# Graph attention in four layers: two of sixteen weight tiles of a unit made by ScalarE and GpSimd

## The chip, the cores and the metric

The kernel runs on one core of a Trainium2 chip. The core has five engines that each work through a queue of their own, in order: PE (TensorE, matrix products), DVE (VectorE), ACT (ScalarE), POOL (GpSimd) and SP, which here issues DMAs. They wait for each other by semaphores. The metric is the device time of one execution in microseconds (us); lower is better.

## The reference

There are 8 batches of 2048 nodes with 64 features, and one adjacency matrix `adj` of 2048 x 2048 zeros and ones. Four layers follow each other, each inside `x = layernorm(x + layer(x, adj))`. Layers 0, 1 and 2 are graph attention:

```python
h = x @ W                                    # layer 0 scales x and normalizes h as well
s1, s2 = h @ a[:64], h @ a[64:]
e = leaky_relu(s1[:, :, None] + s2[:, None, :], 0.2)
att = softmax(where(adj > 0, e, -big), axis=-1)
out = elu(att @ h)                           # layer 0 adds h; layer 2 has relu in place of elu
```

Layer 3 is a softmax per feature over the neighbours, without scores between pairs of nodes. The attention weights, 2048 x 2048 for each batch and each of three layers, are the bulk of the work.

## The kernel before

A **unit** is one layer and one batch. The list `todo` has 24 of them: layers 0 and 1 for batches 0 to 3, then layers 0 and 1 for batches 4 to 7, then layer 2 for all batches. Units are numbered n from 0, so n = 1 to 15 are the units of layers 0 and 1 after the very first; in this text (1,7) is the unit of layer 1 and batch 7. Layer 3 (`l3_products`, `p_l` in the profile) runs between the units of layer 2 and after them.

A unit's weights are made in K = 16 **tiles**: tile `jb` holds 128 source nodes on the partitions and all 2048 target nodes along the free dimension. In layers 0 and 1 a weight is exp of a leaky relu, and as exp(max(a, b)) = max(exp a, exp b), and a factor common to a row cancels in the softmax, a tile is one DVE instruction on exponentials that were taken of vectors before: `max(row, column) * edge`. Here `row` is `s.r` (name `r`, 128 x 2048 fp32, the same values in all partitions), the column is `s.e[:, 1, jb]` (name `se`), and `edge` is the mask as fp8, kept in SBUF. From n = 1 on, `r` lies in PSUM[...]. `spread` puts it there for each unit with four small PE products (`r<-row,ones`) after DVE's last tile of the unit before. In unit 0 the row lies in SBUF.

`weights(u, jb)` issues the DVE instruction into one of four buffers of the name `w`. `products(u, jb)` then issues four PE products of 512 columns (each is two instructions in the profile) that accumulate into `acc` in PSUM. The main loop runs over the units and, inside, over jb. At each jb it calls `reach`, which issues the weights up to this tile, then `products`, then one step of every background generator in `bg` (`bg.step`). These generators do everything else, some pieces at each tile:

- `finish` for the unit just done: ACT copies `acc` to `oT`, PE transposes it (`p_o`), DVE takes reciprocals `den`, ACT scales into `o`, POOL adds (`hb`, `eh`, `o`), ACT squares (`sq_x`), DVE sums (`st_x`), POOL takes a power (`st_x<-isw_x,mhalf`), ACT writes the new rows `x`.
- `scores` and `features0` for units to come: transposes, `h`, `xs`, `y`, scores, exponentials `se`, the row as three bf16 parts `rT3`, which goes to DRAM and comes back as `row`.
- `mask_out`, from unit 9 on: ACT copies the mask to fp32 (`mf`), SP writes it to DRAM for layer 3. The `raw`/`mf` buffers are four of 128 x 1024 each.

All instructions of PE, DVE, ACT and POOL go through a wrapper that keeps the program's order, so that nearly every row of the profile has line 80; one goes by the names of the tiles. Inside an engine the order of the program is the order of execution. The order between engines comes from semaphores, set from which instruction reads or writes which buffer.

Of the kernel before, what the change touches and what calls it, by code (L numbers as in the profile page):

```python
# [8 lines left out]
F32 = mybir.dt.float32  # L9
# [4 lines left out]
I32 = mybir.dt.int32  # L14
AF = mybir.ActivationFunctionType
ALU = mybir.AluOpType
AX = mybir.AxisListType

P = 128
# [31 lines left out]
def gnn4_kernel(ctx: ExitStack, tc: tile.TileContext, t, out):  # L51
    nc = tc.nc
    x_in, adjT = t["x"], t["adjT"]
    B, N, F = x_in.shape
    K = N // P
    K2 = K // 2
# [7 lines left out]
    small = ctx.enter_context(tc.tile_pool(name="small", bufs=2))  # L64
# [42 lines left out]
    class Banks:  # L107
# [4 lines left out]
        pool = None  # L112
        stack = None

        @classmethod
        def use(cls, name, bufs):
            if cls.stack is not None:
                cls.stack.close()
            cls.stack = ExitStack()
            cls.pool = cls.stack.enter_context(tc.tile_pool(name=name, bufs=bufs, space=PSUM))  # L120
# [20 lines left out]
    pe, dve, act, pool = (InOrder(e) for e in (nc.tensor, nc.vector, nc.scalar, nc.gpsimd))  # L141
# [58 lines left out]
    early = early_.enter_context(tc.tile_pool(name="early", bufs=3))  # L200
# [49 lines left out]
    edge = consts.tile([P, K, N], FP8, name="edge")  # L250
# [9 lines left out]
    half_ldeg = consts.tile([P, K], F32, name="half_ldeg")  # L260
    raws = {}

    AT_W = (0, 1, 2, 3, 6, 7, 8, 9)

    def load_raw(jb):

        if jb in AT_W:
            r = work.tile([P, N], I32, tag="w", name=f"raw_{jb}", bufs=4)
            nc.sync.dma_start(r, adjT[jb * P : (jb + 1) * P])
            raws[jb] = [r[:, : N // 2], r[:, N // 2 :]]  # L270
        elif jb < K:
            raws[jb] = []
            for h in range(2):
                r = early.tile([P, N // 2], I32, tag="raw", name=f"raw_{jb}_{h}", bufs=4)
                nc.sync.dma_start(
                    r, adjT[jb * P : (jb + 1) * P, h * (N // 2) : (h + 1) * (N // 2)]
                )
                raws[jb].append(r)
# [31 lines left out]
    def mask_out():  # L310

        for jb in range(K):
            for h in range(2):
                while not 3 < now[2] < K - 1:
                    yield 1
                r = early.tile([P, K2, P], F32, tag="raw", name=f"mf_{jb}_{h}", bufs=4)
                act.copy(
                    r,
                    edge[:, jb, h * (N // 2) : (h + 1) * (N // 2)].rearrange(
                        "p (i c) -> p i c", c=P  # L320
                    ),
                )
                nc.sync.dma_start(
                    mask_d[h * K2 : (h + 1) * K2, :, jb].rearrange("i p c -> p i c"), r
                )
                yield 2
# [22 lines left out]
    for jb in range(4):  # L349
        load_raw(jb)  # L350
# [204 lines left out]
    def exponentials(sc, s1, s2, s, layer, b, n):  # L555

        sc.e = small.tile([P, 3, K], F32, tag="se", name=f"se_{n}", bufs=B + 1)
        for i, v, scale in ((0, s1, 1.0 - ALPHA), (1, s2, ALPHA - 1.0), (2, s2, 1.0)):
            act.activation(sc.e[:, i], v, AF.Exp, scale=scale)

        def top():
            dve.tensor_reduce(
                s_top[:, layer, b : b + 1],
                s,
                AX.XY,
                ALU.max,
                apply_absolute_value=True,
            )

        return top  # L570
# [336 lines left out]
    def unit(layer, b):  # L907
        u = Unit()
        u.layer, u.b, u.n = layer, b, f"{layer}_{b}"
        u.s, u.w = S[layer, b], {}  # L910
        return u
# [4 lines left out]
    def halves(u, jb):  # L916
        parts = 2 if jb in (0, K - 1) and in_psum(u.layer, u.b) else 1
        return [slice(c * (N // parts), (c + 1) * (N // parts)) for c in range(parts)]

    def weights(u, jb):  # L920

        s = u.s
        w = u.w[jb] = work.tile([P, N], F32, tag="w", name=f"w_{u.n}_{jb}", bufs=4)
        low = s.low if u.layer == 2 else s.e[:, 1]
        for sl in halves(u, jb):
            dve.scalar_tensor_tensor(
                w[:, sl], s.r[:, sl], low[:, jb : jb + 1], edge[:, jb, sl], ALU.max, ALU.mult
            )

    def exponential(u, jb):  # L930

        w = u.w[jb]
        for sl in halves(u, jb):
            act.activation(w[:, sl], w[:, sl], AF.Exp, bias=u.s.down[:, jb : jb + 1])

    units, prepared, spreads = [], set(), {0}

    def spread_for(n):
        if n in spreads:
            return  # L940
        spreads.add(n)
        if n == 1:
            Banks.use("psR", 1)
            Banks.r = Banks.pool.tile([P, N], F32, tag="b", name="r")
        spread(*todo[n])
# [3 lines left out]
    def reach(t):  # L949

        while front[0] < K * len(todo):
            n, jb = divmod(front[0], K)
            layer, b = todo[n]
            if n not in prepared or front[0] > t + (2 if layer == 2 else 0):
                break
            if jb == 0:
                spread_for(n)
                units.append(unit(layer, b))
            weights(units[n], jb)
            front[0] += 1  # L960
            if jb == K - 1 and n + 1 in prepared:
                spread_for(n + 1)
        while behind[0] < min(front[0], t + 2):
            n, jb = divmod(behind[0], K)
            if todo[n][0] == 2:
                exponential(units[n], jb)
            behind[0] += 1

    def products(u, jb):

        s, w = u.s, u.w[jb]
        sums = [u.acc[c // 2][F * (c % 2) : F * (c % 2) + F, :] for c in range(NCH)]
        for c in range(NCH):
            pe.matmul(
                sums[c],
                lhsT=s.v[:, jb, :],
                rhs=w[:, c * 512 : (c + 1) * 512],
                start=(jb == 0),
                stop=False,
            )  # L980
        if jb == K - 1:

            assert s.whole
            for c in range(NCH):
                rows = slice(32 * c, 32 * c + 3)
                pe.matmul(sums[c], lhsT=s.mean[rows], rhs=emptyT[rows], start=False, stop=True)
# [341 lines left out]
    todo = [(layer, b) for half in (0, NB) for layer in (0, 1) for b in range(half, half + NB)]  # L1328
# [42 lines left out]
    begin = {0: 2, 1: 3, 4: 4, 5: 5, 6: 6, 8: 7}  # L1371
    for n, (layer, b) in enumerate(todo):
        if (layer, b) == (2, 1):
            early_.close()
            late = ctx.enter_context(tc.tile_pool(name="late", bufs=1))
            bg.add(l3_products())
        if (layer, b) == (2, 5):
            bg.add(flags())
        now[:] = layer, n, 0
        nxt = todo[n + 1] if n + 1 < len(todo) else None  # L1380
        done = nxt is None

        for jb in range(K):
            if n == 0:
                while masks < min(K, 9 + jb):
                    mask(p_deg, masks)
                    masks += 1
                    if masks == K:
                        empties(p_deg)
            now[2] = jb  # L1390
            reach(K * n + jb)
            u = units[n]
            if jb == 0:
                sums_of(u)
            products(u, jb)
            if jb == K - 1:
                end = [lambda u=u: finish(u)]
                if layer < 2:
                    end += [2 if now[0] < 2 else 1, lambda layer=layer, b=b: scores(layer + 1, b)]
                else:  # L1400
                    end += [1, lambda b=b: l3_features(b)]
                if layer == 1 and b % NB == NB - 1:
                    end += [lambda b=b: group(b // NB)]
                bg.add(chain(*end), begun=True)
            elif not done and jb >= 10 and ready(*nxt):
                prepare(*nxt)
                prepared.add(n + 1)
                done = True
            if layer == 0 and jb == 2 and 6 <= b + 4 < B:
                load_x(b + 4)  # L1410
            if n == 0 and jb == 3:
                bg.add(constants())
            if n == 9 and jb == 3:
                bg.add(mask_out())
            if jb == (1 if n < 2 else 4) and n in begin:
                bg.add(features0(begin[n]))
            bg.step()
        while not done:
            bg.step()
            if ready(*nxt):  # L1420
                prepare(*nxt)
                prepared.add(n + 1)
                done = True
# [509 lines left out]
```

## Time and profile before

| | us |
|---|---|
| device time, median of 3 runs (lowest, highest) | 1441.37 (1436.22, 1441.79) |
| the profiled execution, device time | 1439.37 |
| its span, first to last instruction | 1437.6 |
| PE busy in the span | 1238.5 (86%) |
| DVE busy | 1260.6 (88%) |
| ACT busy | 820.3 (57%) |
| POOL busy | 548.0 (38%) |
| units 1 to 15, between the first and the sixteenth spread of `r` | 107 to 781 |

A row of the profile's groups names the engine and operation, the tile written and those read, shapes and count, then busy time, the mean of one in ns, the idle time of the engine just before such instructions, and who ended that idle time. The rows of busy time by stretch give, after the stretch's length, busy us and count of instructions for PE, PE's weight loads, DVE, ACT and POOL, then the granted clock of PE, the share of the DMA engines, and GB/s. Rows of the timeline give start, duration, engine and instruction, several alike merged, and in brackets the idle time before. A busy PE is a model of pipelined products, and so a little generous.

### The profile page before, as it was taken

Reading aid. Unit: us, or ns where it says so; the run is one execution under the profiler, and the core shown is the slowest. Engines: PE = TensorE matmul, PEld = TensorE weight load, DVE = VectorE, ACT = ScalarE, POOL = GpSimd, SP = SyncE. Lnnn points to the kernel's source line nnn. Section 1 sums busy time; section 2 is a strip of 40 time slices with the busy share of each in tenths; the row PEclk is TensorE's granted clock in tenths of the full one; section 3 lists DMA queues with packets and bytes.
Section 4 is the critical chain, followed back from the end, with each engine's and each line's share of the span. In section 5 each row is a group of like instructions: output and inputs, shape, how many; then the busy total and the mean of one; then the engine's idle time right before and its main releaser. Section 6 shows DMA issues by size and latency. Waiting matters only on the chain.

```text
span 1437.6 us, 19117 instructions
## 1 busy us (share of the span) xinstructions
PE 1238.5 (86%) x7138; PEld 620.0 (43%) x7138; DVE 1260.6 (88%) x1260; ACT 820.3 (57%) x1585; POOL 548.0 (38%) x619
## 2 busy tenths in 40 slices
PE   3578788988899988999998887879999898988996
PEld 2323233333233333344332332336665464647996
DVE  4699889997899999999999898898989988878976
ACT  4415444664557545654533986787677766675442
POOL 1152463324423344331322211312445534367665
PEclk9988999999999999999999897999999998989998
DMA  8740000000000022221201000005453354531111
GB/s 297 249 81 1 1 2 1 1 2 1 3 1 1 22 69 88 89 75 53 68 16 37 1 1 15 12 26 150 130 155 101 108 152 116 141 97 46 38 37 33
DMA packets 113335, 90.36 MB, mean 63 GB/s; under 512 B 58077, under 2 KB 91021, under 8 KB 112082
## 3 DMA queue, kind: packets, MB, share of 16 engines
q1 hardware_dynamic: 112690, 87.89, 20.9%
q8 instruction: 58, 0.95, 0.3%
q10 hardware_dynamic: 544, 1.17, 0.2%
q14 instruction: 43, 0.35, 0.1%
HBM read 63.54 MB, written 25.46 MB: 62 GB/s over the span
## 4 chain that ended last, share of the span: by engine, by line
PE 28%; DVE 20%; ACT 8%; issue 5%; POOL 3%; DMA 1%; SPq 0%; POOLq 0%; DVEq 0%; ACTq 0%
PE p_l L80 13%; DVE w L80 12%; PE acc L80 12%; ACT w L80 3%; DVE st_x L80 2%; ACT x L80 2%; DVE o L80 1%; PE p_o L80 1%; ACT sp L80 1%; POOL o L80 1%; PE r L80 1%; DMA mask<-mask_d 1%; DVE x L80 1%; DVE nd L80 1%; DVE fs L80 1%
## 5 line engine op out<-in xcount | busy, mean ns | idle before, releaser
L80 DVE SCALAR_TENSOR_TENSOR w<-r,se,edge 128x2048 f32<-128x2048 f32 (+1 forms) x270 | 555.4, 2103 | 22.0 <-PE r L80 19.2
L80 PE MATMUL acc<-w,pv 128*64 128x512 f32 x2048 | 508.9, 629 | 70.8 <-DVE w L80 63.9
L80 DVE SCALAR_TENSOR_TENSOR w<-r,lo_g,edge 128x2048 f32<-128x2048 f32 (+1 forms) x144 | 298.0, 2095 | 18.1 <-PE r L80 9.7
L80 PE MATMUL acc<-w,x 128*64 128x512 f32 x1024 | 269.1, 656 | 37.0 <-ACT w L80 33.0
L80 ACT ACTIVATE w<-w,down_g 128x2048 f32<-128x2048 f32 (+1 forms) x144 | 257.3, 1809 | 71.2 <-DVE w L80 70.7
L80 PEld LDWEIGHTS p_l<-v,mask 128*128 128x128 f32 x2048 | 253.0, 193 | 65.4 <-issue 52.3
L80 PEld LDWEIGHTS acc<-w,pv 128*64 128x64 f32 x2048 | 133.5, 141 | 337.3 <-issue 190.2
L80 PE MATMUL p_l<-v,mask 128*128 128x256 f32 x2048 | 269.1, 289 | 9.8 <-POOL mask L80 6.3
L80 PEld LDWEIGHTS acc<-w,x 128*64 128x64 f32 x1024 | 68.2, 146 | 163.5 <-issue 92.2
L80 ACT COPY oT<-acc 128x512 f32<-128x512 f32 x48 | 25.8, 589 | 147.5 <-PE acc L80 147.5
L80 ACT ACTIVATE x<-o,st_x 128x64 f32<-128x64 f32 x256 | 90.5, 444 | 1.4 <-DVE st_x L80 1.4
L80 ACT ACTIVATE o<-p_o,den 128x64 f32<-128x64 f32 x256 | 55.9, 326 | 44.9 <-DVE den L80 44.9
L80 ACT ACTIVATE nd<-p_l,empty 128x256 f32<-128x256 f32 x64 | 30.2, 471 | 82.5 <-PE p_l L80 82.4
L80 POOL TENSOR_SCALAR isw_x<-isw_x 128x16 f32<-128x16 f32 x24 | 6.2, 260 | 182.6 <-DVE isw_x L80 171.1
L80 POOL TENSOR_TENSOR st_x<-isw_x,mhalf 128x16 f32<-128x16 f32 x24 | 70.3, 2930 | 2.0
L80 PEld LDWEIGHTS p_o<-rh,oT 128*128 128x128 f32 x384 | 49.7, 196 | 35.9 <-issue 15.4
L80 POOL TENSOR_TENSOR st_h<-isw_h,mhalf 128x16 f32<-128x16 f32 x8 | 23.6, 2952 | 106.7 <-DVE isw_h L80 83.8
L80 PE MATMUL p_o<-rh,oT 128*128 128x130 f32 x384 | 59.9, 293 | 4.6 <-ACT o L80 3.5
L80 DVE RECIPROCAL nd<-nd 128x256 f32<-128x256 f32 x32 | 55.8, 1743 | 0.0
L80 POOL TENSOR_TENSOR eh<-eh,x 128x1024 f32<-128x1024 f32 (+2 forms) x24 | 36.4, 1532 | 45.3 <-ACT eh L80 45.2
L80 POOL COPY x<-x 128x16 f32<-128x16 f32 x16 | 3.3, 205 | 123.8 <-ACT x L80 123.8
L80 PE MATMUL r<-row,ones 3*128 3x512 bf16 x92 | 26.9, 416 | 24.7 <-DVE w L80 23.6
(243 smaller groups left out, 1497.4 us busy)
## 6 DMA issues: line engine op xcount, KB each, us to landing
mask<-mask_d SPq DMA_DIRECT2D x140, 256.0 KB
mask_d<-mf SPq DMA_DIRECT2D x32, 512.0 KB
raw<-in_adjT_dram SPq DMA_DIRECT2D x8, 1024.0 KB
raw<-in_adjT_dram SPq DMA_DIRECT2D x16, 512.0 KB
x<-in_x_dram SPq DMA_DIRECT2D x8, 512.0 KB
x_d<-x SPq DMA_DIRECT2D x8, 512.0 KB
e<-x_d SPq DMA_DIRECT2D x64, 64.0 KB
out_dram<-o SPq DMA_DIRECT2D x64, 64.0 KB
```

The lines of the kernel that those rows point to most:

```text
L80: ins = f(*args, **kwargs)
```

## The change

In units 1 to 15, tiles 6 and 12 are no longer made by DVE. `aside` makes them in two halves of 1024 columns: ACT computes relu(row - column) from the row in PSUM into a buffer `off` in SBUF, POOL adds the column, and POOL multiplies by the mask. As relu(r - c) + c = max(r, c), the result is the same weight. `ASIDE` says when this is issued: tile 6 just before DVE's tile 1, tile 12 just before DVE's tile 7. The negative column is a small POOL instruction more for each unit (`minus`). The products read each 512 columns of these tiles from the two halves.

The buffers move: a pool `raws` holds the four buffers for the loads of the adjacency matrix and is closed at the start of unit 1; a pool `stage` then takes its place, with two halves `off`, and two buffers `mf` for `mask_out` in place of four.

```diff
+    class Stage:
+        stack = ExitStack()
+        pool = None
+        @classmethod
+        def use(cls, name):
+            cls.stack.close()
+            if name:
+                cls.pool = cls.stack.enter_context(tc.tile_pool(name=name, bufs=1))
+    Stage.use("raws")
...
-                r = early.tile([P, N // 2], I32, tag="raw", name=f"raw_{jb}_{h}", bufs=4)
+                r = Stage.pool.tile([P, N // 2], I32, tag="raw", name=f"raw_{jb}_{h}", bufs=4)
...
-                r = early.tile([P, K2, P], F32, tag="raw", name=f"mf_{jb}_{h}", bufs=4)
+                r = Stage.pool.tile([P, K2, P], F32, tag="mf", name=f"mf_{jb}_{h}", bufs=2)
...
+        if (layer, b) != (0, 0):
+            sc.minus = small.tile([P, K], F32, tag="minus", name=f"minus_{n}", bufs=5)
+            pool.tensor_scalar(sc.minus, sc.e[:, 1], -1.0, None, ALU.mult)
...
+    ASIDE = {6: 1, 12: 7}
+
+    def aside(u, jb):
+        s = u.s
+        u.w[jb] = []
+        for h in range(2):
+            sl = slice(h * (N // 2), (h + 1) * (N // 2))
+            y = Stage.pool.tile([P, N // 2], F32, tag="off", name=f"off_{u.n}_{jb}_{h}", bufs=2)
+            act.activation(y, s.r[:, sl], AF.Relu, bias=s.minus[:, jb : jb + 1])
+            pool.tensor_scalar(y, y, s.e[:, 1, jb : jb + 1], None, ALU.add)
+            pool.tensor_tensor(y, y, edge[:, jb, sl], ALU.mult)
+            u.w[jb] += [y[:, :512], y[:, 512:]]
+
+    def set_aside(n):
+        return todo[n][0] < 2 and n > 0
...
-            weights(units[n], jb)
+            if set_aside(n):
+                for late_jb, start in ASIDE.items():
+                    if start == jb:
+                        aside(units[n], late_jb)
+            if not (set_aside(n) and jb in ASIDE):
+                weights(units[n], jb)
...
-                rhs=w[:, c * 512 : (c + 1) * 512],
+                rhs=w[c] if isinstance(w, list) else w[:, c * 512 : (c + 1) * 512],
...
         if (layer, b) == (2, 1):
+            Stage.use(None)
             early_.close()
...
+        if n == 1:
+            Stage.use("stage")
```

## The prediction

> **What bounds the kernel now.** I read the shares of the page first, then the costliest groups, then busy time by stretch, cut at the moments when a unit's row is spread into PSUM (the PE rows `r<-row,ones`, found on the timeline), and last the timeline of one unit. The change touches units 1 to 15 of layers 0 and 1, which the timeline puts at 107 to 781 us, 674 us for 15 units or 44.9 us each.
>
> From the page, the shares and the two groups that make up these units (busy us, mean ns of one, then the idle time before them and who ended it):
> ```profile
> PE 1238.5 (86%) x7138; PEld 620.0 (43%) x7138; DVE 1260.6 (88%) x1260; ACT 820.3 (57%) x1585; POOL 548.0 (38%) x619
> ...
> L80 DVE SCALAR_TENSOR_TENSOR w<-r,se,edge 128x2048 f32<-128x2048 f32 (+1 forms) x270 | 555.4, 2103 | 22.0 <-PE r L80 19.2
> L80 PE MATMUL acc<-w,pv 128*64 128x512 f32 x2048 | 508.9, 629 | 70.8 <-DVE w L80 63.9
> ```
> DVE waits 22 us for others in front of its weight tiles; PE waits 64 us for those tiles. DVE leads, PE follows. By stretch, for units (1,1) and (1,7) and for all fifteen:
> ```profile
> core 0: us, PE busy (x) PEld busy (x) DVE busy (x) ACT busy (x) POOL busy (x), PEclk, DMA share, GB/s
> 293.00:342.00 49.00, 41.53 (x190) 15.69 (x189) 41.84 (x36) 26.27 (x89) 17.73 (x27) 0.93 0.01 2
> 740.00:781.00 41.00, 36.76 (x178) 13.52 (x178) 39.88 (x30) 15.85 (x47) 8.22 (x8) 1.00 0.00 1
> 107.00:781.00 674.00, 603.47 (x3070) 232.35 (x3069) 626.19 (x513) 345.90 (x1023) 251.34 (x264) 0.96 0.09 26
> ```
> DVE is busy 93% of the stage (626 of 674), PE 90%, ACT 51%, POOL 37%. So ACT and POOL have room, and PE stands only (626-603)/15 = 1.5 us a unit behind DVE. Unit (1,7) in order of time (start us, us, engine, row):
> ```profile
> 740.02 1.02 PE L80 MATMUL r<-row,ones 3*128 3x512 bf16 x4 [0.20 <-DVE w L80]
> 741.08 4.74 DVE L80 SCALAR_TENSOR_TENSOR w<-r,se,edge 128x1024 f32<-128x1024 f32 x3 [1.11 <-PE r L80]
> 743.28 1.07 ACT L80 COPY oT<-acc 128x512 f32<-128x512 f32 x2 [6.42 <-PE acc L80]
> 744.24 5.41 ACT L80 ACTIVATE x<-o,st_x 128x64 f32<-128x64 f32 x16
> ...
> 753.19 11.35 DVE L80 SCALAR_TENSOR_TENSOR w<-r,se,edge 128x2048 f32<-128x2048 f32 x5
> ...
> 757.83 1.94 PE L80 MATMUL acc<-w,pv 128*64 128x512 f32 x8 [0.32 <-DVE w L80]
> 759.51 2.37 POOL L80 TENSOR_TENSOR o<-o,eh 128x1024 f32<-128x1024 f32 x1
> ```
> The reader is to see that DVE runs on from tile to tile, five tiles in 11.35 us (2.27 each), without waiting for anyone, that PE needs 1.94 us a tile, and that at a unit's start DVE is already two tiles in when PE has just finished the unit before (ACT's `oT` copy waits for that). This lead is what the change costs.
>
> [...] Before, no ACT row reads `r`[...]; but the changed program, as built, keeps the two apart by semaphores (below). [...] the trace has 2.36 to 2.38 us for `o<-o,eh` and `o<-o,hb`. [...] the trace has 1.93 us for a POOL cast of 128x2048, so 0.97 for 1024. [...] unit 0's last tile, with its row in SBUF, took 4.30 us beside a POOL product at 107 us where 2.34 is usual, while the tiles from the PSUM row never exceed 2.35 us. So I expect no contention from the new POOL work.
>
> **The change, part by part** (per unit unless said; tile j means the j-th of sixteen).
> - Removed: DVE's tiles 6 and 12, 2 x 2.27 = 4.5 us. Were nothing added, 15 x 4.5 = 68 us.
> - Added on ACT: four relus of 128x1024 from PSUM. Nearest row: `eh<-o`, 1.07 us, so 4.3 us; the 128x512 PSUM copy takes 0.54 in a pair, which agrees.
> - Added on POOL: four additions of a column (0.97 to 1.3 us, I take 1.2) and four products with the mask (2.37), 14.3 us, and the 0.26 us `minus`. POOL goes from 16.8 to 31.4 us a unit: it has the room, but each tile is a block of 7.1 us that other POOL work stands behind.
> - Moved on no queue: the DMAs of SP are the same. `mf` has two buffers in place of four, so ACT's copy waits for the write before last. DMA moved 104 to 109 GB/s while these wrote, so one 512 KB write takes some 4.9 us, against a copy every two tiles (4.5 us). Zero to 2 us for each of 32, nothing likely: a tile pair becomes slower.
> - PE: the same products. Nothing.
> - **The new waits.** In the built program DVE's tile 1 waits in all fifteen units for the second relu of tile 6, and its tile 7 for the second relu of tile 12; before, these waited for no ScalarE work. [...] Behind the waiting row stands all of DVE's queue, and PE waits for DVE's next tile. In turn the relus of tile 6 stand on ACT behind `oT`, so behind PE's end of the last unit, and those of tile 12 wait for PE's products of tile 6, because `off` has just the two half buffers.
>
> Tile 1: the row is spread at 0 (741.05 above). DVE's tile 0 ends at 2.5. `oT` runs 2.3 to 3.3, two relus end at 5.4. DVE starts tile 1 at 5.5 in place of 2.5: 3.0 us where the relus follow `oT` directly (five units by the program's order), 5.7 in (1,7), where eight `x` rows (2.7 us) come between, others between these. I take 4.0, less 0.8 for small DVE rows that fill the gap: 3.2.
>
> Tile 7: from the end of DVE's tile 5, PE needs 1.94 for tile 5, 1.9 for tile 6, then ACT 1.06 for the second relu and some 0.2 of signalling: 5.1 us with DVE still. If ACT's queue is late (feature rows `xs`, `x`, `y` stand ahead, 1.4 us per four), more. I walked four units with the durations of their own rows in the order of the new program: idle of 5.3 us in (1,7), 6.8 in (0,5), 7.9 in (1,0), 11 in (1,1), of which half in the last was idle later before. I take 7.0, less 0.7 of small rows: 6.3.
>
> Later: POOL's block for tile 12 starts only then, at about 25 us into the unit, and `o<-o,eh` (18.5 us in, above) ends behind it at some 35. DVE's `st_x` sum stands in its queue before the last tiles and waits for that: 1.7 us in (1,7) and (1,0), I take 1.5.
>
> Sum: -4.5 + 3.2 + 6.3 + 1.5 = +6.5 us. The four walks give whole units of 51 (41 before), 47 (40), 51 (43) and 55 (49): +10, +7, +8, +6, mean 7.7. I take **+7.0 us a unit, between the two, 15 x 7 = +105 us**. On the profiled execution's own time of 1439.4 us (span 1437.6 and 1.8 around it) this is 1544; that run lies 2.0 below the median of those shown (1441.4), so no correction is worth making.
>
> Ends of the unknown costs: both waits at their least (3.0 - 1.0 and 5.1 - 1.0) and nothing later give 15 x 1.6 = +24; with ACT late as in (1,1) in most units and `mf` waiting, 15 x 11 = +165.
>
> **Rivals.** (a) *A small loss.* The waits cost little more than the tile pair saves, as DVE's old idle (48 us of the stage) is absorbed by the new: +10 to +45 us, 1450 to 1485. For it: `st_x` and the row spread already cost idle. Against it: 5.1 us at tile 7 is a chain of PE and ACT times that no slack shortens. (b) *Faster.* DVE keeps its lead because ACT is far ahead, so both waits are over when DVE comes, and PE becomes the bound: of 68 us, PE's 1.5 us a unit of distance and its 70 us of waits leave about 40, so 1400. For it: ACT is idle 49% of the stage and waits 6.4 us for PE at `oT`. Against it: ACT waits there exactly for PE, and relus behind it cannot run earlier. It decides for this side if the two waits together stay under 4.5 us. (c) *POOL becomes the bound*: blocks of 7.1 us end after PE wants the tile. At 31 of 45 us POOL is not full, but where its features, `pow` (2.9 us) and `hb` come first, tile 6 may be late and everything after it: +11 us a unit, 1604. (d) *It does not do what it says*: excluded, since the built program has 120 POOL rows and 60 relus more and 30 DVE tiles fewer.
>
> **How the numbers follow.** The main case, +45 to +165 us, has 0.84; (a) 0.09, of which a third falls within 0.5%, which is about what a measurement of this kernel can tell from no change (7 us); (b) 0.05; beyond (c)'s end 0.02. The range of 1485 to 1604 is the main case's. Faster 0.05, same 0.03, slower 0.92.
>
> **What would show it.** In the changed profile: the `w<-r` group idle before it 100 to 180 us, released by ACT `off`, in place of 22; DVE's share of the stage near 75%, its stage about 780 us long; pieces of idle near 3 to 6 us at tile 1 and 5 to 8 us at tile 7; POOL near 470 us in the stage; PE's idle before `acc` up by about the loss; the stage after, with layer 2, unchanged. I am wrong if DVE's waits for `off` stay under 60 us in all, or if PE waits longer for POOL `off` than DVE for ACT `off`.

## The result, and the profile after

The changed kernel takes **1593.82 us**, median of four runs (1588.27 to 1597.31), beside 1441.58 for the kernel before in runs taken with it (1436.22 to 1445.37). The ratio is 1.108, 95% interval 1.105 to 1.111: slower by 152 us. The profiled execution took 1597.3 us with a span of 1595.5, which is 157.9 us more than the span before.

The same rows of the page as before, with the new ones (busy us, mean ns of one, idle time before them and who ended it):

```profile
PE 1292.7 (81%) x7138; PEld 634.8 (40%) x7138; DVE 1217.0 (76%) x1230; ACT 881.8 (55%) x1645; POOL 841.5 (53%) x754
...
L80 PE MATMUL acc<-w,pv 128*64 128x512 f32 x1808 | 506.1, 698 | 173.8 <-DVE w L80 166.5
L80 DVE SCALAR_TENSOR_TENSOR w<-r,se,edge 128x2048 f32<-128x2048 f32 (+1 forms) x240 | 488.0, 2073 | 187.8 <-ACT off L80 160.1
...
L80 POOL TENSOR_SCALAR off<-off,se 128x1024 f32<-128x1024 f32 x60 | 170.8, 2847 | 119.8 <-ACT off L80 119.8
...
L80 POOL TENSOR_TENSOR off<-off,edge 128x1024 f32<-128x1024 f32 x60 | 120.5, 2009 | 5.0
...
L80 ACT ACTIVATE off<-r,minus 128x1024 f32<-128x1024 f32 x60 | 63.5, 1113 | 14.3 <-PE acc L80 4.9
...
L80 DVE TENSOR_REDUCE st_x<-o 128x16 f32<-128x1024 f32 x24 | 29.1, 1214 | 51.0 <-POOL o L80 51.0
```

DVE has 30 tiles less, and its idle time in front of the others went from 22 to 188 us, 160 of it ended by ACT's `off`. The sum `st_x<-o` of the unit just done now stands 51 us waiting for POOL. In the kernel before, its row was:

```profile
L80 DVE TENSOR_REDUCE st_x<-o 128x16 f32<-128x1024 f32 x24 | 29.0, 1210 | 14.5 <-POOL o L80 14.5
```

Busy time of the stage, between the first and the sixteenth spread of `r`:

```profile
core 0: us, PE busy (x) PEld busy (x) DVE busy (x) ACT busy (x) POOL busy (x), PEclk, DMA share, GB/s
108.00:940.00 832.00, 661.99 (x3068) 248.95 (x3069) 582.08 (x483) 407.56 (x1083) 544.36 (x398) 0.87 0.07 21
```

The stage takes 832.5 us in place of 674.0, and that is the whole loss; what follows the sixteenth spread takes 655 us in place of 656. DVE was busy 93% of the stage and is now 70%; no other engine is busier than PE's 80%. So nothing has become a bound by its work: the engines stand in each other's queues. DVE's waits in the stage (us in total, times, longest):

```profile
DVE w L80 <- ACT off L80: 160.1, 30, 10.0
DVE st_x L80 <- POOL o L80: 51.0, 14, 6.3
DVE w L80 <- PE r L80: 25.7, 11, 4.8
```

Thirty waits for `off`, two in each of 15 units. Unit (1,7), which took 41 us, takes 54. From its timeline:

```profile
889.50 1.07 ACT L80 COPY oT<-acc 128x512 f32<-128x512 f32 x2 [6.16 <-PE acc L80]
...
890.46 2.77 ACT L80 ACTIVATE x<-o,st_x 128x64 f32<-128x64 f32 x8
...
893.12 2.10 ACT L80 ACTIVATE off<-r,minus 128x1024 f32<-128x1024 f32 x2
...
895.25 2.35 DVE L80 SCALAR_TENSOR_TENSOR w<-r,se,edge 128x2048 f32<-128x2048 f32 x1 [5.48 <-ACT off L80]
...
897.66 3.13 PE L80 MATMUL acc<-w,pv 128*64 128x512 f32 x8 [4.49 <-DVE w L80]
...
901.65 3.63 PE L80 MATMUL acc<-w,pv 128*64 128x512 f32 x8 [0.87 <-DVE w L80]
...
911.50 1.89 PE L80 MATMUL acc<-off,pv 128*64 128x512 f32 x8
...
912.63 2.12 ACT L80 ACTIVATE off<-r,minus 128x1024 f32<-128x1024 f32 x2 [1.18 <-issue]
...
914.78 6.87 DVE L80 SCALAR_TENSOR_TENSOR w<-r,se,edge 128x2048 f32<-128x2048 f32 x3 [5.89 <-ACT off L80]
...
923.65 2.34 POOL L80 TENSOR_TENSOR o<-o,eh 128x1024 f32<-128x1024 f32 x1
...
926.03 1.22 DVE L80 TENSOR_REDUCE st_x<-o 128x16 f32<-128x1024 f32 x1 [4.38 <-POOL o L80]
```

Read from above: `oT`, eight rows `x`, two relus, and only then DVE's tile 1, after 5.5 us of idle time. After PE's first products of tile 6 (`acc<-off`) come the relus of tile 12, and DVE's tile 7 after 5.9 us. Then POOL's `o`, late behind POOL's four instructions for tile 12, and DVE's sum after 4.4 us. PE stands idle 4.5 us at the first of these, and its next eight products take 3.1 and 3.6 us in place of 1.94.

### The profile page after: what moved, and what is told of

Its sections match the earlier page's. It is cut to its first block, busy times and chain, and to the rows that moved or that the text cites. A ratio compares the mean times of both kernels' runs of the same rounds, so it can differ in the third digit from the quotient of the medians.

```text
span 1595.5 us, 19328 instructions
## 1 busy us (share of the span) xinstructions
PE 1292.7 (81%) x7138; PEld 634.8 (40%) x7138; DVE 1217.0 (76%) x1230; ACT 881.8 (55%) x1645; POOL 841.5 (53%) x754
## 4 chain that ended last, share of the span: by engine, by line
PE 37%; DVE 22%; ACT 14%; POOL 11%; issue 4%; DMA 1%; SPq 0%; POOLq 0%; DVEq 0%; ACTq 0%
PE acc L80 21%; DVE w L80 14%; PE p_l L80 11%; POOL off L80 5%; ACT off L80 3%; ACT w L80 3%; POOL o L80 2%; DVE st_x L80 2%; ACT x L80 2%; PE p_o L80 2%; PE r L80 1%; DVE o L80 1%; ACT sp L80 1%; ACT oT L80 1%; PE p_s L80 1%
## 5 line engine op out<-in xcount | busy, mean ns | idle before, releaser
L80 DVE SCALAR_TENSOR_TENSOR w<-r,se,edge 128x2048 f32<-128x2048 f32 (+1 forms) x240 | 488.0, 2073 | 187.8 <-ACT off L80 160.1
L80 PEld LDWEIGHTS acc<-w,pv 128*64 128x64 f32 x1808 | 129.0, 153 | 443.2 <-DVE w L80 223.1
L80 PE MATMUL acc<-w,x 128*64 128x512 f32 x1024 | 265.2, 646 | 38.5 <-ACT w L80 34.4
L80 POOL TENSOR_SCALAR off<-off,se 128x1024 f32<-128x1024 f32 x60 | 170.8, 2847 | 119.8 <-ACT off L80 119.8
L80 POOL TENSOR_TENSOR off<-off,edge 128x1024 f32<-128x1024 f32 x60 | 120.5, 2009 | 5.0
L80 ACT ACTIVATE off<-r,minus 128x1024 f32<-128x1024 f32 x60 | 63.5, 1113 | 14.3 <-PE acc L80 4.9
L80 DVE TENSOR_REDUCE st_x<-o 128x16 f32<-128x1024 f32 x24 | 29.1, 1214 | 51.0 <-POOL o L80 51.0
L80 ACT ACTIVATE sq_x<-o 128x1024 f32<-128x1024 f32 x24 | 25.4, 1057 | 66.9 <-POOL o L80 62.3
```

The source lines that it names most:

```text
L80: ins = f(*args, **kwargs)
```

## Experiments

The runs of the kernel before beside these experiments had medians of 1442.2, 1437.7 and 1441.1 us, single ones 1433 to 1446. Most of the experiments are single runs, so differences under some 10 us are not read. "Stage" is always the time between the first and sixteenth spread.

**1. What the relus read.** The relu's source alone is changed (the banks named below are the row's place in PSUM):

```diff
-            act.activation(y, s.r[:, sl], AF.Relu, bias=s.minus[:, jb : jb + 1])
+            act.activation(y, edge[:, jb, sl], AF.Relu, bias=s.minus[:, jb : jb + 1])
```

> The four relus of a unit read the mask in SBUF in place of the row in PSUM, so tiles 6 and 12 get other values; ACT, POOL and PE do the same work at the same places, but ACT and DVE no longer read the same banks. Theory (DVE waits because ACT reads the banks of its row): DVE's 160 us of waiting for ACT 'off' go to under 10, and the time falls to 1400-1480 us; PE may then wait for POOL 'off' in some units. Rival (POOL's blocks of 9.7 us a tile, or ACT's late queue, bound the units whoever reads what): the time stays above 1550, and the wait moves from DVE to PE, which waits over 100 us for POOL 'off'. Rival (contention: POOL's new work lengthens DVE rows): DVE busy in the stage stays at 582 us and the time at 1500-1550.

Measured: 1555.0 us, stage 787.7. DVE does not wait for `off` at all any more, 160 us gone, and yet only 39 us are won. The theory that ACT's reading of the row is the loss falls in this form. The first rival has its time, above 1550, but not its wait, since PE waits 0.9 us for POOL's `off`. DVE's busy time, 576 us, stays near the 582 that the second rival named. DVE's two longest waits in this run's stage:

```profile
DVE st_x L80 <- POOL o L80: 124.2, 14, 12.9
DVE s L80 <- POOL st_h L80: 26.4, 5, 7.9
```

The time reappears at another place of the same queue. Unit (1,6) of this run:

```profile
818.84 2.85 POOL L80 TENSOR_SCALAR off<-off,se 128x1024 f32<-128x1024 f32 x1 [0.77 <-ACT off L80]
...
821.77 2.00 POOL L80 TENSOR_TENSOR off<-off,edge 128x1024 f32<-128x1024 f32 x1
...
823.75 2.85 POOL L80 TENSOR_SCALAR off<-off,se 128x1024 f32<-128x1024 f32 x1
826.68 2.00 POOL L80 TENSOR_TENSOR off<-off,edge 128x1024 f32<-128x1024 f32 x1
828.63 2.34 POOL L80 TENSOR_TENSOR o<-o,eh 128x1024 f32<-128x1024 f32 x1
...
831.01 1.22 DVE L80 TENSOR_REDUCE st_x<-o 128x16 f32<-128x1024 f32 x1 [11.49 <-POOL o L80]
```

POOL's block for tile 12 occupies 9.8 us, `o` comes behind it, and DVE, no longer late, stands 11.5 us at the sum with all its tiles queued behind. In the changed kernel the wait for `off` had hidden most of this.

**2. One tile at a time, and a later start.** Three edits of one line:

```diff
-    ASIDE = {6: 1, 12: 7}
+    ASIDE = {6: 1}            # only six
+    ASIDE = {12: 7}           # only twelve
+    ASIDE = {5: 1, 12: 8}     # later start
```

> Only tile 6 is made by ACT and POOL, tile 12 by DVE again. The prediction's sum, with the waits as measured: tile 1 costs 3.7 us of DVE's waiting a unit (55 us in all) against one tile of 2.27 us saved (34 us): 1441 + 20 to + 50 = 1460-1490 us, with about 55 us of DVE waiting for 'off', all of it at tile 1. Rival (the two waits are one late queue: what is not waited at tile 7 is waited elsewhere, or the clock of PE is what costs): over 1520.

Measured: 1488.8 us; 53.2 us of waits for `off`, one in each unit, 3.5 us each. The upper end of what was expected. DVE waits 22.9 us at `st_x`.

> Only tile 12 is made by ACT and POOL, its relus issued ahead of DVE's tile 7; tile 6 is made by DVE. The prediction's chain at tile 7 was: the relus wait for PE's products of tile 6 because 'off' has two half buffers. Here nothing holds 'off' any more, since the only earlier user is the unit before. If the buffer is what makes tile 7 wait, the wait falls from 7.0 us a unit to 2-3 us (two relus of 1.1 us), 30-45 us in all, and the time is 1440-1480. If ACT's queue (feature rows ahead of the relus, which wait for PE or POOL themselves) is what makes it wait, it stays at 5-7 us a unit, 75-105 us in all, and the time is 1500-1540.

Measured: 1522.9 us, the time of the queue theory; 65.5 us of waits for `off`, 4.4 each, between the two theories. The least, twice 2.19 us, are the two relus themselves; the longest are 8.2 and 8.4. The wait at `st_x` is 54.6 us, as long as in the full change: it is mainly tile 12's block on POOL that holds up `o`.

> Tiles 5 and 12 in place of 6 and 12, the second begun at tile 8 in place of 7: PE has finished with the 'off' halves of tile 5 two tiles before ACT needs them, in place of none. Buffer theory: the second wait falls from 7.0 us a unit to 2-3, the DVE wait for 'off' from 160 us to about 90-100, the time to 1510-1550. ACT queue theory: the second wait stays near 6-7 us, the DVE wait at 140-170, the time within 15 us of 1594. The tile after it has less time, so PE may wait for POOL 'off' (9.7 us a tile, four DVE tiles are 9.1 us): up to 2 us a unit, 30 us.

Measured: 1592.0 us, the time of the queue theory. The wait at the second tile falls from 7.0 to 5.5 us a unit, again between; the time does not fall, and the wait at `st_x` grows from 51 to 61.5 us. PE's products of tile 5 were over more than 2 us before the second pair of relus in every unit, so the 5.5 us are the relus (2.2) and what stood ahead of them on ACT.

In the trace of the full change the two reasons can be told apart. In seven of the 15 units the first relu of tile 12 starts 0.10 to 0.11 us after PE has ended the products of tile 6's first half: there the buffer `off` holds it. In the other eight it starts 0.4 to 5.1 us after them and straight behind other work of ACT: there ACT's queue holds it. DVE waits 6.2 us on average in the seven and 7.6 in the eight.

**3. Without GpSimd's work.** ACT makes the half tile in one pass, from the row in PSUM, and in a second kernel from the mask:

```diff
-            act.activation(y, s.r[:, sl], AF.Relu, bias=s.minus[:, jb : jb + 1])
-            pool.tensor_scalar(y, y, s.e[:, 1, jb : jb + 1], None, ALU.add)
-            pool.tensor_tensor(y, y, edge[:, jb, sl], ALU.mult)
+            act.activation(y, s.r[:, sl], AF.Identity, bias=s.e[:, 1, jb : jb + 1])           # no pool work
+            act.activation(y, edge[:, jb, sl], AF.Identity, bias=s.e[:, 1, jb : jb + 1])      # neither
```

> The four half tiles of a unit are made by ACT alone (row plus column, one pass, read from PSUM as in the change), GpSimd's additions and mask products are left out, so tiles 6 and 12 have other values. [...] Theory (two waits: DVE for ACT's relu on its banks, and DVE's st_x sum for POOL 'o' behind POOL's blocks; the second is 51 us in the changed kernel, 14.5 before): st_x falls to about 15 us, the waits for 'off' stay at 140-180 us, and the time is 1530-1570. Rival (POOL work as such slows the rest, through contention with DVE or late features): under 1510. Rival (bank waits are all there is): 1585-1600.

Measured: 1541.7 us, as the theory of two waits had it. DVE's waits in the stage:

```profile
DVE w L80 <- ACT off L80: 155.8, 30, 10.0
...
DVE st_x L80 <- POOL o L80: 21.4, 7, 6.3
```

The waits for `off` are those of the change (160), so POOL has no part in them; tile 7 alone has 7.1 us a unit. The next run, which differs from this one in what ACT reads, has no such wait: 155.8 us here, none there. So the wait comes with ACT and DVE both reading `r`, which this program orders one after the other; no run leaves that order out, so what the two would do without it is not shown.

> As the one before, and ACT reads the mask in SBUF in place of the row: neither the shared banks nor POOL's blocks are left, while DVE still makes two tiles less in a unit and ACT four passes more (values of tiles 6 and 12 are others). Theory (the two waits together are the loss; the relu run alone has shown that each hides behind the other): waits for 'off' under 10 us, st_x under 20 us, and the 68 us of removed tiles show, less what PE then waits: 1375-1420. Rival (something else, as ACT's extra 64 us or the lower clock of PE, costs too): over 1440.

Measured: 1434.2 us. The theory's number and the rival's (over 1440) are both missed: both causes are gone, but the gain over the kernel before (1437.7 beside this run) is 3 us, less than a single run can show. The wait at `st_x` is 55 us, not under 20.

**4. What two tiles less are worth.** The products of tiles 6 and 12 read two buffers filled once:

```diff
+        if not fixed:
+            for h in range(2):
+                y = Stage.pool.tile([P, N // 2], F32, tag="off", name=f"off_{h}", bufs=2)
+                pool.memset(y, 1.0)
+                fixed.extend([y[:, :512], y[:, 512:]])
+        u.w[jb] = fixed
```

> Tiles 6 and 12 are made by nobody: their products read two buffers filled once with ones, so the result is another; ACT, POOL and DVE have no work in their place. This measures what two DVE tiles less in a unit are worth by themselves; 68 us by the count of the prediction. Theory (the run with neither wait gave only 3 us because the rest of the chain, PE's products and the sums of the unit before, leaves no more once DVE is relieved): 1410-1440, with DVE waiting 40-60 us for POOL 'o' at its st_x sum. Rival (there the gain was eaten by ACT's four passes more, 64 us of an engine that is 51% busy): 1370-1400.

Measured: 1408.2 us, so 33 us for 68 us of DVE work. The time lies between the theory's band, which ends at 1410, and the rival's, which ends at 1400. Busy time of the stage of this run, then of the run with neither (columns as above):

```profile
107.00:753.00 646.00, 590.51 (x3073) 233.37 (x3070) 558.58 (x484) 345.95 (x1023) 258.17 (x281) 0.96 0.10 27
```
```profile
107.00:776.00 669.00, 599.33 (x3073) 236.41 (x3070) 559.32 (x484) 406.10 (x1083) 256.19 (x279) 0.94 0.09 27
```

With two tiles less PE is busy 91% of the stage and DVE 86%: DVE now waits 38.9 us at `st_x` (14.5 before) and 29.7 for the spread row (19.2 before), 35 us more together, which is what the 68 us lose. The only work added from the first line to the second is 60 us of ACT, on an engine 54% busy; it costs another 26 us, so the rival had a part of the reason. PE does not wait for these passes. DVE's wait at `st_x` grows by 16 us, and POOL's waits for ACT's `o` and `eh` by 12; that the steps towards `o` stand behind the new passes in ACT's queue is the likely reason, but it was not tested apart.

**5. The sum issued later.** In the kernel with neither wait, in that of experiment 1, and in the full change, one line of `finish`:

```diff
             pool.tensor_tensor(o, o, e, ALU.add)
             e_slots.give()
-            yield 2
+            yield 5
```

> As the run with neither wait (values of tiles 6 and 12 are others), and DVE's sum st_x of the unit before is issued three tiles later, so that DVE comes to it when POOL's 'o' is there. Theory (the sum's place in DVE's queue holds the gain of the removed tiles back): st_x falls from 55 us to under 20, the time from 1434 to 1395-1415. Rival (PE is the bound: 599 us busy of 669 at a clock of 0.94): the idle turns up elsewhere, at the row's spread or at free buffers w, and the time stays at 1425-1440.

Measured: 1430.0 us. `st_x` waits 0.3 us instead of 55, and the time stays: the rival. The wait for the spread row went from 25 to 49 us, as the next rows come later.

> As the run whose relus read the mask in place of the row (values of tiles 6 and 12 are others; POOL's blocks as in the change, no shared banks), and st_x issued three tiles later. There DVE waited 124 us at st_x for POOL 'o', behind POOL's block of tile 12. Theory (that wait is how POOL's blocks cost 121 us): st_x falls to 30-60 us, the time from 1555 to 1470-1510. Rival (POOL's blocks hold up everything that follows in the unit, features and rows too, so moving the sum only moves the wait): 1530-1560.

Measured: 1517.3 us, 38 less than in experiment 1, between the two. `st_x` falls from 124 to 16 us; 30 come back at the spread row (25.6 to 55.6) and 15 at `st_x` behind POOL's power. So the place of the sum is about a third of what POOL's blocks cost; the rest moves on.

> The full change, and st_x issued three tiles later. In the change DVE waits 51 us at st_x and 160 us for 'off'. Theory (each of the two waits takes up part of what the other would cost; GpSimd off alone gave 1542): st_x falls under 25 us, 'off' stays at 150-185, the time is 1560-1580. Rival (they add): 1555 or less. Rival (no effect, for the waits for 'off' grow by as much): 1588-1598.

Measured: 1591.6 us: no effect, though not by the rival's reason. The wait of 51 us is gone, `off` falls to 146, but the wait for the row rises from 26 to 45 us and DVE's busy time from 582 to 601.

**6. The rest of the change.** With `ASIDE = {}` only the pools, the two buffers `mf` and `minus` remain.

> Only what else the change brings along: the new pools with two buffers mf in place of four, and the small POOL product 'minus'; DVE makes all sixteen tiles. The prediction put mf at nothing likely, at most 2 us for each of 32, and the small product at 0.26 us on an engine with room: 1439-1447, the same within what can be measured. If mf waited for its writes in most cases: up to 1500.

Measured: ratio 1.0007, interval 0.9988 to 1.0027. They cost nothing that can be measured.

**7. A version meant to avoid both waits.** Tile 6 alone, its relus issued at the spread, in turn with the halves of DVE's tile 0; ACT adds the column:

```diff
-            act.activation(y, s.r[:, sl], AF.Relu, bias=s.minus[:, jb : jb + 1])
-            pool.tensor_scalar(y, y, s.e[:, 1, jb : jb + 1], None, ALU.add)
-            pool.tensor_tensor(y, y, edge[:, jb, sl], ALU.mult)
+            so = slice((1 - h) * (N // 2), (2 - h) * (N // 2))
+            act.activation(y, s.r[:, sl], AF.Relu, bias=s.minus[:, jb : jb + 1])
+            dve.scalar_tensor_tensor(
+                w[:, so], s.r[:, so], s.e[:, 1, 0:1], edge[:, 0, so], ALU.max, ALU.mult
+            )
...
+        for y, e, sl in u.rest:
+            act.activation(y, y, AF.Identity, bias=e)
+            pool.tensor_tensor(y, y, edge[:, jb, sl], ALU.mult)
```

> A version without either wait, with tile 6 alone set aside: its two relus are issued right after the row's spread, ahead of oT on ACT, each on the two banks that DVE's tile 0 (made in two halves) is not reading; ACT adds the column, and POOL only multiplies by the mask, after the scores' steps of the first tile. Expected: DVE waits for 'off' under 25 us in all in place of 53 with tile 6 alone, st_x near 15 us; DVE makes one tile less a unit, 34 us, of which PE, 1.5 us a unit behind DVE, lets pass about 20: 1410-1435, faster than before. Rival (ACT is late at the spread because the last unit's rows stand ahead, so that tile 0 waits): 1440-1470. Rival (oT's bank copy comes late, and PE waits for acc): PE's wait for oT over 30 us, 1450-1480.

Measured: 1477.6 us, ratio 1.026 (1.021 to 1.031). It is slower than the kernel before, for a reason that neither rival had. Unit (1,7) of this run:

```profile
778.26 1.02 PE L80 MATMUL r<-row,ones 3*128 3x512 bf16 x4 [0.20 <-DVE w L80]
...
779.32 1.11 ACT L80 ACTIVATE off<-r,minus 128x1024 f32<-128x1024 f32 x1 [4.22 <-PE r L80]
780.46 1.28 DVE L80 SCALAR_TENSOR_TENSOR w<-r,se,edge 128x1024 f32<-128x1024 f32 x1 [2.26 <-ACT off L80]
...
781.78 1.11 ACT L80 ACTIVATE off<-r,minus 128x1024 f32<-128x1024 f32 x1 [1.35 <-DVE w L80]
...
782.93 1.28 DVE L80 SCALAR_TENSOR_TENSOR w<-r,se,edge 128x1024 f32<-128x1024 f32 x1 [1.18 <-ACT off L80]
```

ACT and DVE take turns even where they read different halves of the row: in these rows each starts 0.03 to 0.04 us after the other has ended. The order of this program holds for the tile `r` as a whole, so each half tile of DVE waits for a relu, 68 us in all. Some 20 us of these stand in place of the wait for the spread row (20.7 with tile 6 alone in experiment 2, none here). Two tiles `r` of 1024 columns each, or four half buffers `off`, were not tried.

**The price of each cause.** Each kernel of this ladder differs from the one above it in one cause, apart from the pools and `minus`, which experiment 6 put at nothing:

| | us | step |
|---|---|---|
| before | 1441.6 | |
| two DVE tiles less, nothing in their place | 1408.2 | -33 |
| and ACT's four passes, from the mask | 1434.2 | +26 |
| and these read the row in PSUM | 1541.7 | +107 |
| and GpSimd adds and multiplies (the change) | 1593.8 | +52 |

Taken in the other order, GpSimd's work costs 121 us (1434.2 to 1555.0) and the row in PSUM 39 on top. Alone they would be 107 and 121, together they are 160: each hides part of the other. That ranks them no further than this, and it says why undoing either alone disappoints.

## Why the prediction was right, and by how much it was short

The direction and the main mechanism held, and 1593.8 lies in the range, 10 us inside its upper end and 50 us above the number. DVE's own time in the stage shows the steps that were short. Predicted were -68 us of tiles, +142 of waits for `off`, +22 at `st_x`, 97 in all (the number took 105, between this and four walks). Measured were -68, +160, +36.5, and two terms that were priced at nothing: +24 us of DVE busy time and +6.5 at the spread row; 159 in all, against a stage longer by 158.5.

- *The new waits.* Tile 1: 3.2 predicted, 3.7 measured; tile 7: 6.3 predicted, 7.0 measured (4.8 to 10.0). The walked units show that this was more than luck: idle at tile 7 of 5.3, 6.8, 7.9 and 11 us was predicted for (1,7), (0,5), (1,0) and (1,1), and 5.9, 6.5, 7.5 and 10.0 came; the whole units took 54.2, 48.5, 55.1 and 60.1 us in place of 51, 47, 51 and 55. That they come with ACT's reading of the row is shown by experiments 1 and 3: with the row not read by ACT they are gone (160.1 us to none), without POOL's work they stay (155.8). They come as well where the two read different halves (experiment 7). That the relus of tile 12 wait for `off` holds in seven units of 15; in the other eight it is ACT's late queue, which was offered as an "if".
- *Removed: 4.5 us a unit.* The instructions follow each other at 2.27 us, as said, but their time is worth 33 us, not 68. The sum took DVE as the bound for the whole gain; with the tiles left out, half of it turns up as DVE's waits at `st_x` and for the spread row, with PE busy 91% of the stage. The rival of a faster kernel, which put the gain at 40, had the right size for this term.
- *ACT's relus.* 1.11 us, predicted 1.07. But ACT was taken as having room, and its passes from the mask cost 26 us, likely through the steps of the last unit that queue behind them.
- *POOL.* The addition of a column was put at 1.2 us from a cast and took 2.85; the product was put at 2.37 and took 2.01. A tile is 9.7 us, not 7.1, and POOL has 544 us in the stage, not 470. Accordingly "later, 1.5 us a unit" was 2.4, and experiment 1 shows 7.3 (124.2 less 14.5, over 15) lying ready behind the other wait. That so low a price of POOL moved the sum by only 0.9 us a unit was luck.
- *"I expect no contention from the new POOL work"* failed. The large tiles kept 2.34 us each, as argued, but the small DVE rows did not. The first pair of lines is from the kernel before, the second from the change:

```profile
L80 DVE SCALAR_TENSOR_TENSOR st_x<-st_x 128x16 f32<-128x16 f32 x24 | 4.6, 192 | 0.8 <-POOL st_x L80 0.8
L80 DVE TENSOR_TENSOR s<-h,st_h 128x32 f32<-128x32 f32 x8 | 1.8, 220 | 0.5 <-POOL st_h L80 0.5
```
```profile
L80 DVE SCALAR_TENSOR_TENSOR st_x<-st_x 128x16 f32<-128x16 f32 x24 | 12.6, 524 | 0.8 <-POOL st_x L80 0.8
L80 DVE TENSOR_TENSOR s<-h,st_h 128x32 f32<-128x32 f32 x8 | 6.3, 788 | 2.2 <-POOL st_h L80 2.2
```

  Without POOL's work (experiment 3) the first is 187 ns again, and DVE is busy 559 us in the stage in place of 582. So the step from 1541.7 to 1593.8 is 24 us of slower DVE rows and 30 at `st_x` (51.0 less 21.4). All 15 small DVE rows of the stage that took over 1 us ran beside a POOL instruction on two tensors, eleven of them beside the new products, and ended 0.02 to 0.08 us after it. The timeline of the change has one of them:

```profile
343.45 2.01 POOL L80 TENSOR_TENSOR off<-off,edge 128x1024 f32<-128x1024 f32 x1
343.73 1.76 DVE L80 SCALAR_TENSOR_TENSOR st_x<-st_x 128x16 f32<-128x16 f32 x1
```

  The prediction's argument rested on the tiles alone. The kernel before has a small row of this kind: `beyond<-beyond,fext` took 1.82 us beside POOL's `pv` at 105 us, and 0.16 just before it.
- *PE: nothing.* The same products are busy 662 us in place of 603, at a granted clock of 0.87 in place of 0.96. In the timeline of (1,7), after 4.5 us idle, the next two groups of eight products took 3.13 and 3.63 us, and the granted clock from 897.6 to 905.3 us was 0.56; then twenty-four took 5.37 at 1.00. After 2.8 us idle before tile 7, eight kept 1.94. What sets the clock was not tested, and what the lower clock adds to the time apart from the waits was not separated.
- *mf: nothing likely.* Confirmed (1.0007).
- *POOL as the bound* (1604 predicted) is near in number and wrong in mechanism: no PE product of the stage waits for POOL's `off`. What costs is what stands behind POOL's blocks in its queue, and the DVE rows that they slow.

## What to carry to other kernels

Before moving work off a busy engine, measure what its absence alone is worth, with the result left out: here 33 us of 68, a ceiling that any of the new costs could break. Work moved to another engine of the same chain must be placed with regard to what stands behind it there and to what both engines read; idle percentage says nothing of either (ACT was busy 51% of the stage, POOL 37%, before work moved to them). And where two waits stand in one in-order queue, the one that shows covers the other: undo both before pricing one.

## Not expected of the hardware

- GpSimd's addition of an fp32 column, in place, took 2.85 us for 128x1024 fp32, longer than its product with an fp8 mask (2.01) or its sum of two fp32 tiles (2.35).
- Small DVE instructions of 0.16 to 0.3 us took up to 1.9 us beside GpSimd's new products, while DVE's tiles of 2.34 us from the row in PSUM did not change.
